# Graph attention over two layers: a chunk's exponentials added by DMA before one summing matmul, and a different pace for layer 1

## The chip, the cores and the metric

The kernel runs on one core of a Trainium2 chip. The metric is the device time of one launch in microseconds. The core has five engines with their own instruction queues, each worked off in order: TensorE (PE, with its weight loads shown as PEld), VectorE (DVE), ScalarE (ACT), GpSimd (POOL) and SyncE (SP), which here only issues DMAs. They meet through semaphores. TensorE writes into PSUM; all other data lies in SBUF, and DMAs move it between SBUF and the device's memory, or within SBUF.

## What is computed

The input is x (8 graphs of 2048 nodes with 256 features) and one adjacency matrix adj of 2048 x 2048. Layer 0 is masked multi-head attention with 4 heads of 64, in chunks of 256 keys, followed by two normalisations. Layer 1 is a graph attention layer with one head. Cut to what matters:

```python
# layer 0; scores in chunks of 256 keys, softmax over each chunk by itself
scores = einsum('bhnd,bhjcd->bhnjc', q, kc) / sqrt(64)
scores = where(mask == 0, -10.0, clip(scores, -10.0, 10.0))
attn = softmax(scores, axis=-1)            # over the 256 keys of one chunk
ctx = einsum('bhnjc,bhjcd->bhnd', attn, vc)  # added up over the chunks
out = layernorm(ctx @ Wo.T + bo + x) * gamma + beta
h = layernorm(x + out)
# layer 1
Wh = h @ W
e = leaky_relu((Wh @ a1)[:, :, None] + (Wh @ a2)[:, None, :], 0.2)
attention = softmax(where(adj > 0 or i == j, e, -inf), axis=-1)
result = layernorm(h + elu(attention @ Wh))
```

Since each chunk of layer 0 has a softmax of its own, each chunk needs the sum of its 256 exponentials for every query and head, the inverse of that sum, and a multiplication of its 64 values per head by that inverse before it is added to the context.

## The kernel before

Everything is in float32, and the instructions of all engines are written out by hand in the order in which they run. The order is built in *beats*. One beat is one tile of 128 keys of layer 0 against a block of 512 queries; two beats are a chunk (`J`, with `half` 0 and 1), 8 chunks a block of queries, 4 blocks a batch (graph), 8 batches: 256 chunks, 512 beats. After them the loop at line 986 adds beats in which layer 1 runs alone; there are 592 in all.

A beat of layer 0 has, in the program's order:

- `begin_beat` (line 816): for the steps of layer 1 in flight, the exponential of the weights on ACT (727) and their addition into `acc` on GpSimd (736); then new steps are taken from `layer1()` as the credit allows, each with an addition on ACT (714); then line 718 on VectorE.
- the scores of two pairs of heads, `sc`, on TensorE (899) into two PSUM tiles of [128, 2, 512]; the clip and mask on VectorE (909); the exponentials `e` on ACT (912) into SBUF tiles of a pool with 8 buffers, four for a chunk.
- `middle_of_beat`: the mask of layer 1's edges on VectorE (723).
- for the chunk before (`prev`): in half 0 the sums ("part 2", with a matrix of ones) and the first 32 values of every head, in half 1 the other 32 values (928). Each part takes 8 matmuls, for 4 heads and 2 key tiles. In the trace each matmul is two records, so a part has 16. The four heads use 32 columns of the array each. ACT copies each result to SBUF (936, 942).
- the sums' chain: `ds` on ACT (942), a DMA that rearranges it into `dc` (944), the reciprocal on VectorE (950), a DMA to device memory (952), a broadcast DMA back into `r` (956), and two beats after the sums the multiplication of the values on VectorE (963) and the addition into `ctxT` on GpSimd (964). `agenda` holds what is to run at the end of which beat. In the first batch the chain is given longer (`early`).
- `end_beat` (842): layer 1's products on TensorE (746, 761 in the last batch), then one step of each generator in `ahead` and `fins`: the preparation of layer 1 for the next batch (`prelude`, with the row maxima of line 438), the end of layer 0 for a block (`fin`), the end of layer 1 for a block (`fin1`), projections.

A step of layer 1 is one tile of 128 keys against 512 queries; 16 steps are a block, four blocks a batch. `begin_beat` adds 1.5 to the credit (1.3 in the last batch of layer 0, 1.0 after it), keeps at most 2, and takes a step for each whole credit. When the next block isn't ready, `layer1()` yields `None` and no step is taken in that beat. A block thus takes about 10.7 beats (12.3 in the last batch). Layer 1 of a batch runs beside layer 0 of the next batches, once layer 0 has finished all its blocks: it is at work in 45 beats of 64, from beat 89 on.

The tiles `w` of the steps have five buffers, and `hx`, `hr` and `ex` of `fin1` one each. `fin1` loads `hr` when the block ends, scales and exponentiates in the next beat, takes the minimum and maximum, and adds `hr` on GpSimd in the beat after (600 to 611).

Of the kernel before, what the change touches and what calls it, by code (L numbers as in the profile page):

```python
# [28 lines left out]
def tile_adj_attention__then__gat(  # L29
# [62 lines left out]
    eight = ctx.enter_context(tc.tile_pool(name="eight", bufs=8))  # L92
# [136 lines left out]
    for n in range(2):  # L229
        t = one.tile([P, F], F32, tag=("hx", "ex")[n], name=f"a_bc{n}")  # L230
        nc.sync.dma_start(out=t, in_=a[n * F : (n + 1) * F, :].rearrange("f o -> (f o)").partition_broadcast(P))
        a_bc.append(t)
# [284 lines left out]
    def last_prelude(b):  # L517
# [35 lines left out]
        while "hT" not in st:  # L553
# [4 lines left out]
            if beat >= 2 * total + 2 and held is None:  # L558
                held = []
                for n in range(HT):  # L560
                    fr = eight.tile([P, 2, HN], BF16, tag="e", name=f"far{b}_{n}")
# [26 lines left out]
    def fin1(b, ib, hx, acc):  # L588

        hr = one.tile([P, TPB, F], F32, tag="hr", name=f"hr{b}_{ib}")  # L590
        nc.sync.dma_start(out=hr, in_=h_d[b, ib])
# [10 lines left out]
        ex = one.tile([P, TPB, F], F32, tag="ex", name=f"ex{b}_{ib}")  # L602
        nc.scalar.activation(ex, hx, AF.Exp, bias=shifts[:, 1:2])
        yield
        nc.vector.scalar_tensor_tensor(hx, ex, 1.0, hx, ALU.min, ALU.max)
        nc.gpsimd.tensor_add(hx, hx, hr)
# [6 lines left out]
    def fin1_last(b, ib, hx):  # L613
# [4 lines left out]
        ex = one.tile([P, TPB, F], F32, tag="ex", name=f"ex{b}_{ib}")  # L618
# [181 lines left out]

    l1 = layer1()
# [5 lines left out]
    credit = 0.0  # L807
    RATE, LAST_RATE = 1.5, 1.3
# [7 lines left out]
    def begin_beat(rate):  # L816
# [5 lines left out]
        credit = min(credit + rate, 2.0)  # L822
        while l1_live and credit >= 1.0:
            s = next(l1, False)
            if s is False:
                l1_live = False
            elif s is None:
                break
            else:
                credit -= 1.0  # L830
                lows.append(s)
                s.low()
        for s in leaking:
# [36 lines left out]

    prev = None
    mk0 = {}
    for J in range(total + 1):
# [4 lines left out]
        cur = {"b": b, "ib": ib, "j": j, "es": [], "ctxT": ctxT, "v": vs[min(b, B - 1)], "name": f"{b}_{ib}_{j}"}  # L878
        for half in range(2):
# [13 lines left out]
            begin_beat(RATE if b < B - 1 else LAST_RATE)  # L893
            if live:
                scs = []
# [14 lines left out]
                for hp in range(NPAIR):  # L910
                    e = eight.tile([P, 2, IB], F32, tag="e", name=f"e{b}_{ib}_{c}_{hp}")
                    nc.scalar.activation(e, scs[hp], AF.Exp)  # L912
                    cur["es"].append(e)
            middle_of_beat()

            early = J < NIB * NCH
            if prev is not None:
                if half == 0:

                    pool, tag = (one, "hr") if early and J % 3 == 2 else (two, "un")  # L920
                    prev["un"] = pool.tile([P, 2, IB], F32, tag=tag, name=f"un{prev['name']}")
                for part in ((2, 0), (1,))[half]:
                    m = ps_m.tile([P, IB], F32, tag="m", name=f"u{prev['name']}_{part}")
                    for i in range(2):
                        pc = 2 * prev["j"] + i
                        for h in range(H):
                            f0 = h * D + part * DH
                            nc.tensor.matmul(  # L928
                                m[h * DH : (h + 1) * DH, :],
                                prev["v"][pc // TPB][:, pc % TPB, f0 : f0 + DH] if part < 2 else ones[:, 0:DH],  # L930
                                prev["es"][2 * i + h // 2][:, h % 2, :],
                                start=(i == 0),
                                stop=(i == 1),
                            )
                    if part < 2:
                        nc.scalar.copy(prev["un"][:, part, :], m)  # L936
                    else:

                        ds = two.tile([P, IB], F32, tag="ds", name=f"ds{prev['name']}")
                        nc.scalar.copy(ds, m)  # L942
# [92 lines left out]
```

## Time and profile before

| | |
|---|---|
| median of 3 runs | 4392.25 us (4391.52 to 4399.52) |
| the profiled execution | 4387.29 us, span 4385.5 us |
| granted TensorE clock, mean | 0.98 |
| DMA | 415.63 MB, mean 95 GB/s, hardware queue 30.5% of 16 engines |
| last exponential of layer 0 | about 4115 us |

Line numbers in a profile's rows are those of the kernel. In a row of instructions, "out<-in" names the tiles written and read, "xN" the number of records, then come the busy time and the mean of one in ns, and what the engine sat idle for before them. A row of the sums over windows has the window's bounds and length, then busy time and records of each engine, the granted clock, the DMA engines' busy share and GB/s. A busy TensorE is not TensorE at its peak, since the ends of its pipelined matmuls are modelled.

### The profile page before, as it was taken

The numbers are of one execution on the slowest core, as the hardware profiler recorded it, in microseconds if no ns is written. First come the engines' busy times: TensorE is split into PE (matmuls) and PEld (weight loads), VectorE is DVE, ScalarE is ACT, GpSimd is POOL, SyncE is SP. The second block draws the span as 40 slices with busy tenths as digits, with TensorE's granted clock in tenths as the row PEclk, the third lists the DMA queues.
The fourth block names the chain that finished last, engine by engine and source line by source line (L and its number), as shares of the span: only waits on it lengthen the run. The fifth ranks groups of instructions, "written<-read, shape, count | busy, mean of one in ns | idle before, by whom it ended". The sixth has DMA issues, their size and how long they took to land. (4 is left out here: it accounts for less than half of the span.)

```text
span 4385.5 us, 61171 instructions
## 1 busy us (share of the span) xinstructions
PE 4064.2 (93%) x23053; PEld 1907.6 (43%) x23053; DVE 3417.7 (78%) x4530; ACT 2564.4 (58%) x3842; POOL 1760.5 (40%) x901
## 2 busy tenths in 40 slices
PE   8889989999999999999899999999999999899767
PEld 3223334454344534454344543445434454344456
DVE  5876589965998669976699766996579965888777
ACT  5655556665566556666566665566556665555546
POOL 0222235543455334444245442554325542354420
PEclk9999999999999999999999999999999999999889
DMA  5554232222332233321333223232232222322321
GB/s 166 182 163 149 71 115 86 83 73 89 99 90 81 64 107 102 100 75 51 105 102 98 74 74 105 85 95 78 70 106 85 89 78 67 115 83 80 123 73 58
DMA packets 257641, 415.63 MB, mean 95 GB/s; under 512 B 85440, under 2 KB 120512, under 8 KB 256448
## 3 DMA queue, kind: packets, MB, share of 16 engines
q1 hardware_dynamic: 257344, 411.71, 30.5%
q8 instruction: 181, 2.97, 0.3%
q14 instruction: 116, 0.95, 0.1%
HBM read 340.66 MB, written 68.88 MB: 93 GB/s over the span
## 5 line engine op out<-in xcount | busy, mean ns | idle before, releaser
L912 ACT ACTIVATE e<-sc 128x1024 f32<-128x1024 f32 x1024 | 1034.2, 1020 | 1049.9 <-DVE sc L909 1006.7
L909 DVE SCALAR_TENSOR_TENSOR sc<-sc,mk 128x1024 f32<-128x1024 f32 x1024 | 1206.7, 1223 | 538.3 <-PE sc L899 352.6
L899 PE MATMUL sc<-qT,kT 64*128 64x512 f32 x4096 | 1060.4, 633 | 86.7 <-ACT e L912 86.2
L964 POOL TENSOR_TENSOR ctxT<-ctxT,un 128x1024 f32<-128x1024 f32 x224 | 568.5, 2538 | 1145.3 <-DVE un L963 1007.0
L928 PE MATMUL u<-e,v 128*32 128x512 f32 x8192 | 980.9, 597 | 0.0
L746 PE MATMUL us<-wh,w 128*128 128x256 f32 x3584 | 878.6, 395 | 81.9 <-ACT w L727 60.4
L746 PEld LDWEIGHTS us<-wh,w 128*128 128x128 f32 x3584 | 667.7, 193 | 422.2 <-ACT w L727 110.7
L736 POOL TENSOR_TENSOR acc<-acc,w 128x512 f32<-128x512 f32 x392 | 601.7, 1535 | 544.9 <-ACT w L727 534.4
L899 PEld LDWEIGHTS sc<-qT,kT 64*128 64x128 f32 x4096 | 347.2, 189 | 611.6 <-ACT e L912 281.8
L718 DVE SCALAR_TENSOR_TENSOR w<-ab,sj,w 128x512 f32<-128x512 f32 x512 | 571.5, 1137 | 4.6 <-ACT w L714 4.5
L928 PEld LDWEIGHTS u<-e,v 128*32 128x32 f32 x8192 | 240.6, 110 | 659.7 <-issue 543.9
L928 PE MATMUL u<-e,ones 128*32 128x512 f32 x4096 | 497.5, 604 | 0.0
L723 DVE TENSOR_TENSOR w<-w,mk 128x512 f32<-128x512 f32 x512 | 458.6, 917 | 37.1 <-DMA mk<-mask 34.6
L438 DVE CUSTOM_DVE_ANT_0 fb<-sj_row,fb 128x1024 bf16<-128x1024 f32 x240 | 387.8, 1626 | 2.3 <-DMA fb<-far 2.3
L714 ACT ACTIVATE w<-ab,sj 128x512 f32<-128x512 f32 x512 | 352.2, 714 | 8.7 <-POOL acc L734 5.4
L727 ACT ACTIVATE w<-w 128x512 f32<-128x512 f32 x512 | 308.8, 629 | 75.9 <-DVE w L723 75.3
L936 ACT COPY un<-u 128x512 f32<-128x512 f32 x512 | 300.5, 587 | 66.5 <-PE u L928 57.6
L963 DVE TENSOR_TENSOR un<-un,r 128x1024 f32<-128x1024 f32 x224 | 278.1, 1242 | 42.2 <-DMA r<-rd 36.7
L928 PEld LDWEIGHTS u<-e,ones 128*32 128x32 f32 x4096 | 107.8, 110 | 356.5 <-issue 305.4
L950 DVE RECIPROCAL dc<-dc 128x16 f32<-128x16 f32 x256 | 63.9, 249 | 149.8 <-DMA dc<-ds 134.0
L942 ACT COPY ds<-u 128x512 f32<-128x512 f32 x256 | 148.5, 580 | 3.0 <-PE u L928 2.5
L349 POOL TENSOR_TENSOR y<-x,bo_bc 128x1024 f32<-128x1024 f32 x32 | 77.6, 2426 | 163.6 <-DMA x<-in_x_dram 103.0
(112 smaller groups left out, 3114.7 us busy)
## 6 DMA issues: line engine op xcount, KB each, us to landing
r<-rd SPq DMA_DIRECT2D x256, 256.0 KB
mk<-mask SPq DMA_DIRECT2D x120, 512.0 KB
fb<-far SPq DMA_DIRECT2D x240, 256.0 KB
xT_k<-in_xT_dram SPq DMA_DIRECT2D x32, 512.0 KB
raw<-in_adjT_dram SPq DMA_DIRECT2D x32, 512.0 KB
rawf<-in_adj_dram SPq DMA_DIRECT2D x32, 512.0 KB
x<-in_x_dram SPq DMA_DIRECT2D x32, 512.0 KB
h_d<-y SPq DMA_DIRECT2D x32, 512.0 KB
```

Of the source, the lines that this page charges most:

```text
L438: nc.vector.tensor_tensor_reduce(out=fb, in0=row, in1=fb, scale=1.0, scalar=2 * FAR * 0.999, op0=ALU.add, op1=ALU.max, accum_out=dst,)
L714: nc.scalar.activation(self.w, k["ab"][:, 1, :], AF.Identity, bias=k["sj"][:, 1, c : c + 1])
L718: nc.vector.scalar_tensor_tensor(self.w, k["ab"][:, 0, :], k["sj"][:, 0, c : c + 1], self.w, ALU.add, ALU.max)
L723: nc.vector.tensor_tensor(self.w, self.w, self.k["mks"][self.c // HT][:, self.c % HT, :], ALU.min)
L727: nc.scalar.activation(self.w, self.w, AF.Exp)
L736: nc.gpsimd.tensor_add(k["acc"], k["acc"], self.w)
L746: nc.tensor.matmul(k["us"][:, t, :], self.w[:, ts(t, P)], k["wh"][c // TPB][:, c % TPB, 0:F], start=(first and t % 2 == 0), stop=last, ski ...
L899: nc.tensor.matmul(sc[:, h, :], kTs[b][c // TPB][h * D : (h + 1) * D, hp, ts(c % TPB, P)], qT[h * D : (h + 1) * D, hp, :], start=True, sto ...
L909: nc.vector.scalar_tensor_tensor(scs[hp], scs[hp], -CLIP, cap, ALU.max, ALU.min)
L912: nc.scalar.activation(e, scs[hp], AF.Exp)
L928: nc.tensor.matmul(m[h * DH : (h + 1) * DH, :], prev["v"][pc // TPB][:, pc % TPB, f0 : f0 + DH] if part < 2 else ones[:, 0:DH], prev["es"] ...
L964: nc.gpsimd.tensor_add(p["ctxT"], p["ctxT"], p["un"])
```

## The change

Where layer 1 has steps in flight at the start of the two beats in which a chunk's values are made (`beside`), the two key tiles of its exponentials are added by two DMAs, issued from GpSimd, one for each pair of heads: `es[0] += es[2]`, `es[1] += es[3]`. They are issued after the second half of the chunk's values. The sum over keys is then made from the two resulting tiles with 4 matmuls instead of 8, at the start of a half 1 beat, two beats after the DMAs and three after the beat in which the sums were made before. The reciprocal and its two DMAs come in the middle of the beat after that, and the scaling two beats after the sums; `last_scaled` keeps the scalings of successive chunks in successive beats. Where layer 1 isn't at work, the sums stay in half 0, now after the first values, with 8 matmuls.

The tiles of the exponentials have fixed places: `e{J % 2}_{(half + J // 2) % 2}_{hp}`, eight in all as before. A chunk's half 0 takes the places of the half 1 tiles of the chunk two before, that is of the sources of the additions.

The credit is counted in thirds: 4 a beat beside layer 0, 3 after it, at most 6, and it is cleared when a block has ended or isn't ready. A block takes 12 beats. In all there are 594 beats.

The room in SBUF is shared out anew: `ds` has one buffer instead of two, `un` three instead of two, and `ex` of `fin1` takes the tile of `hr`, so that `hr` is loaded after `ex` has been read, and added one beat later. In `fin1_last`, `ex` takes the tile `x`.

```diff
-    eight = ctx.enter_context(tc.tile_pool(name="eight", bufs=8))
...
-        hr = one.tile([P, TPB, F], F32, tag="hr", name=f"hr{b}_{ib}")
-        nc.sync.dma_start(out=hr, in_=h_d[b, ib])
         yield
...
-        ex = one.tile([P, TPB, F], F32, tag="ex", name=f"ex{b}_{ib}")
+        ex = one.tile([P, TPB, F], F32, tag="hr", name=f"ex{b}_{ib}")
         nc.scalar.activation(ex, hx, AF.Exp, bias=shifts[:, 1:2])
         yield
         nc.vector.scalar_tensor_tensor(hx, ex, 1.0, hx, ALU.min, ALU.max)
+        hr = one.tile([P, TPB, F], F32, tag="hr", name=f"hr{b}_{ib}")
+        nc.sync.dma_start(out=hr, in_=h_d[b, ib])
+        yield
         nc.gpsimd.tensor_add(hx, hx, hr)
...
-    RATE, LAST_RATE = 1.5, 1.3
...
-        credit = min(credit + rate, 2.0)
-        while l1_live and credit >= 1.0:
+        credit = min(credit + thirds, 6)
+        while l1_live and credit >= 3:
             s = next(l1, False)
             if s is False:
                 l1_live = False
             elif s is None:
+                credit = 0
                 break
             else:
-                credit -= 1.0
+                credit -= 3
                 lows.append(s)
                 s.low()
+                if s.c == NT - 1:
+                    credit = 0
...
+    def sums(p):
+        m = p["m"] = ps_m.tile([P, IB], F32, tag="m", name=f"s{p['name']}")
+        tiles = 1 if p["added"] else 2
+        for i in range(tiles):
+            for h in range(H):
+                nc.tensor.matmul(
+                    m[h * DH : (h + 1) * DH, :],
+                    ones[:, 0:DH],
+                    p["es"][2 * i + h // 2][:, h % 2, :],
+                    start=(i == 0),
+                    stop=(i == tiles - 1),
+                )
+    def inverses(p, early):
+        nonlocal last_scaled
+        ds = one.tile([P, IB], F32, tag="ds", name=f"ds{p['name']}")
+        nc.scalar.copy(ds, p.pop("m"))
...
+        lag = 1 if early else 0
+        if p["added"] and live:
+            at(-(beat + 1), inverse)
+        else:
+            at(beat + lag, inverse)
+        last_scaled = max(beat + 2 + 2 * lag, last_scaled + 1)
+        at(last_scaled, scaled)
...
-            begin_beat(RATE if b < B - 1 else LAST_RATE)
+            early = J < NIB * NCH
+            if half == 0:
+                beside = prev is not None and live and bool(lows or edged or weighted)
+            if half == 1:
+                for p in unsummed:
+                    sums(p)
+            begin_beat(4)
+            if half == 1:
+                for p in unsummed:
+                    inverses(p, False)
+                unsummed = []
...
-                    e = eight.tile([P, 2, IB], F32, tag="e", name=f"e{b}_{ib}_{c}_{hp}")
+                    e = one.tile(
+                        [P, 2, IB],
+                        F32,
+                        tag=f"e{J % 2}_{(half + J // 2) % 2}_{hp}",
+                        name=f"e{b}_{ib}_{c}_{hp}",
+                    )
                     nc.scalar.activation(e, scs[hp], AF.Exp)
                     cur["es"].append(e)
+            for fn in agenda.pop(-beat, []) if beat else []:
+                fn()
             middle_of_beat()
             if prev is not None:
                 if half == 0:
-                    pool, tag = (one, "hr") if early and J % 3 == 2 else (two, "un")
-                    prev["un"] = pool.tile([P, 2, IB], F32, tag=tag, name=f"un{prev['name']}")
-                for part in ((2, 0), (1,))[half]:
...
+                    prev["un"] = three.tile([P, 2, IB], F32, tag="un", name=f"un{prev['name']}")
+                values(prev, half)
+                if half == 0 and not beside:
+                    sums(prev)
+                    inverses(prev, early)
+                if half == 1 and beside:
+                    for hp in range(NPAIR):
+                        nc.gpsimd.dma_start(out=prev["es"][hp], in_=prev["es"][NPAIR + hp], accum_op=ALU.add)
+                    prev["added"] = True
+                    unsummed.append(prev)
...
-        begin_beat(1.0)
+        begin_beat(3)
```

`values(p, part)` holds the matmuls of one part of the values and their copy, and `inverse` and `scaled` the same operations as before; `spread`, the broadcast DMA, is now the end of `inverse`.

## The prediction

> **What bounds the kernel now.** The page gives shares of the whole span; the stages are told apart by the sums over windows. The exponentials of line 912 count the beats, two to a beat, so the window from 1145 to 1541 us, with 90 of them, is 45 beats beside layer 1, and the next 130 us are 19 beats without it. The pair repeats every 64 beats.
>
> ```profile
> PE 4064.2 (93%) x23053; PEld 1907.6 (43%) x23053; DVE 3417.7 (78%) x4530; ACT 2564.4 (58%) x3842; POOL 1760.5 (40%) x901
> ...
> 1145.00:1541.00 396.00, 383.36 (x2158) 191.37 (x2151) 328.47 (x413) 240.95 (x363) 191.47 (x102) 1.00 0.27 81
> 1541.00:1671.00 130.00, 118.75 (x734) 44.70 (x730) 87.25 (x131) 74.81 (x114) 42.10 (x19) 0.99 0.34 106
> ...
> 3791.00:4113.00 322.00, 300.33 (x1726) 141.41 (x1718) 266.93 (x350) 188.77 (x288) 145.45 (x75) 0.98 0.28 84
> 4113.00:4386.00 273.00, 190.85 (x773) 147.08 (x771) 220.71 (x375) 139.12 (x237) 60.87 (x34) 0.85 0.26 87
> ```
>
> The columns are length, then PE, PEld, DVE, ACT and POOL busy. Beside layer 1 TensorE is busy 383.4 of 396 us (97%), VectorE 83%. Without layer 1 it is 118.75 of 130, or 6.25 us of TensorE a beat and 4.6 of VectorE (87.25/19). TensorE sets the time until 4113 us; only the tail, where layer 1 runs alone, waits for others. Within the first window the groups by form say what TensorE does:
>
> ```profile
> L746 PE MATMUL us<-wh,w 128*128 128x256 f32 x512 | 122.7, 389 | 5.4 <-ACT hx L773 2.9 <-ACT w L727 2.5
> L909 DVE SCALAR_TENSOR_TENSOR sc<-sc,mk 128x1024 f32<-128x1024 f32 x90 | 106.1, 1223 | 42.1 <-ACT w L727 24.0 <-PE sc L899 18.1
> L899 PE MATMUL sc<-qT,kT 64*128 64x512 f32 x360 | 91.3, 625 | 1.4 <-ACT e L912 1.4
> L912 ACT ACTIVATE e<-sc 128x1024 f32<-128x1024 f32 x90 | 90.7, 1020 | 85.1 <-DVE sc L909 81.4
> L928 PE MATMUL u<-e,v 128*32 128x512 f32 x719 | 86.0, 595 | 0.0
> L928 PE MATMUL u<-e,ones 128*32 128x512 f32 x356 | 43.0, 599 | 0.0
> ```
>
> The last row is the target: no idle before it, so each microsecond of it is on the path. The last view is the timeline where the new wait will fall.
>
> ```profile
> 1713.26 1.92 PE L928 MATMUL u<-e,v 128*32 128x512 f32 x16
> ...
> 1715.12 3.72 PE L746 MATMUL us<-wh,w 128*128 128x256 f32 x16
> ...
> 1718.67 3.60 PE L256 MATMUL pq<-xT_q,WT_q 128*128 128x512 f32 x8
> ...
> 1722.20 1.99 PE L899 MATMUL sc<-qT,kT 64*128 64x512 f32 x8
> ...
> 1724.72 2.15 ACT L912 ACTIVATE e<-sc 128x1024 f32<-128x1024 f32 x2 [0.60 <-DVE sc L909]
> ...
> 1729.72 1.99 PE L899 MATMUL sc<-qT,kT 64*128 64x512 f32 x8
> ```
>
> A chunk's second half of values ends at 1715.2 us; the next beat's exponentials start 9.5 us later, and the scores that need their PSUM buffers 14.5 us later.
>
> [...] No GpSimd DMA is in this trace (the queue list has the hardware queue and instruction fetch only), [...] the two edges of line 723 at 1725.73 took 4.85 us beside GpSimd additions, against 0.68 us for one at 1717.50.
>
> **The change part by part.** *Removed.* Over the kernel the sums are 497.5 us for 4096 records, 16 a chunk: 1.94 us. An added chunk keeps 8, so it saves 0.97 us. In the changed program's order GpSimd has 322 new DMAs, two for each of 161 chunks: 24 in each of six full phases, 17 in the last. That is 161 x 0.97 = 156 us of TensorE, all in the 97% stage.
>
> *Moved: layer 1.* At 4/3 steps a beat with the credit cleared, a block takes 12 beats, where it took about 10.7. Following the loop, a phase has 50 beats instead of 45, and 14 are left without layer 1. TensorE per 64 beats was 383.4 + 118.75 = 502.1 us and becomes 502.1 - 23.3 = 478.8. Its idle time was 12.6 and 11.3. Without layer 1 it goes with the beats, 11.3 x 14/19 = 8.3. Beside layer 1 VectorE has 328.5 + 5 x 4.6 = 351 us in a phase of about 401, 87% where it was 83%; the steps per beat are more even. Idle there is between 12.6 (nothing changes) and 40 (VectorE sets every second beat); I take 22, since both engines then stand near full and wait for one another. A cycle is 478.8 + 8.3 + 22 = 509 against 526, 17 us less; six make -102. The last phase saves 17 x 0.97 = 16.5 and loses 3.5 in the same way: -13. The tail gets two beats more (594 in all against 592), at 273/80 = 3.4 us: +7.
>
> *Added: the wait.* The half-0 exponentials of a chunk overwrite the second tiles of the chunk two before, which are the sources of its additions. ACT therefore waits for both DMAs; behind it are the copies of the values and the weights of the next beat, and behind those TensorE. The DMA may start when the second values end. From there to the next scores that need the buffers, TensorE has products for two beats (3 steps in two pairs of three, 2 in the third, 1.96 us each), scores 2.07, values 1.92 and sums 0.97: 10.8 or 8.9 us, less 1.0 for an exponential. So the second addition may land some 9.8 us after the values (7.8 in every third chunk), more where projections stand between.
>
> Its landing is not in the trace. [...] The other transfers hold 27% of the DMA engines, [...] hidden in two chunks of three, 0.8 late in the third, which is 161/3 x 0.8 = 43 us at worst; projections cover about half of these, so +22.
>
> *GpSimd.* [...] Behind them wait the additions of context and of weights; it is busy 191 of 396 us beside layer 1, [...] If the cover went, the five buffers of w would make ACT wait.
>
> *At nothing.* The DMA chain of the inverse gets a beat more between copy and reciprocal, before the edges instead of after; VectorE's waits for it (134 us in total, off the TensorE path now) can only shrink. The inverse's two stores and loads keep their order in SP's queue, but stand ahead of the far load of that beat, which waits for VectorE anyway. One ds buffer: its copy-out is a chunk old. Three un buffers for two: the scaling comes up to three beats later. The shared tag of ex and hr moves a load behind an exponential and the normalisation a beat later; with 12 beats a block that is covered. The e tags are the same eight tiles.
>
> Sum against the profiled execution's 4387.3 us: -102 - 13 + 7 + 22 = -86, so 4301. The median of the runs shown is 5 us above that execution: 4306.
>
> **Rivals.** *All of it is kept*: no idle is added and the additions land in time. -156 - 6 x 3 (idle of the lost beats) + 7 = -167, a median of 4225 at best, 4250 with small losses. For it: the even steps and the inverse's longer lead. Against: VectorE at 87%.
>
> *Another wait takes it*: each phase gains the 23 us again as waits between VectorE and TensorE (idle 45 of 400), and the time stays at 4380 to 4400. For it: line 909 already waits 42 us in a phase. Against: [...] the stretching of lines 718 and 723 does not grow.
>
> *Slower: the additions land late.* Place: ACT's first exponential of each even beat. The gain without lateness is 108 us, so it is used up at 108/161 = 0.67 us per chunk beyond the slack, a landing at about 10.2 us. At 12 us a chunk loses 2.2 us, or 4.2 in every third, 2.1 on average if projections cover some: +338 - 108, or 4622. At 15 us it is over 5000. For it: the rate of an accumulating DMA is unknown, both DMAs share engines with broadcasts of 256 KB, [...] Against: where projections stand between, the slack is longer, 14.5 us to the scores in the timeline above.
>
> *That the change does not do what it says* is excluded by the order: 322 DMAs in, the halved sums out.
>
> **How the numbers follow.** Forecast (4265 to 4350): 0.46. All kept: 0.14. Another wait: 0.11, half of it within 0.2%. Late additions: 0.29. What a measurement of this kernel can tell from no change is about 0.2%, 9 us. So faster 0.65, same 0.06, slower 0.29. The range is 4235 to 4540: it leaves out some 0.17 of the late cases and 0.03 of the best; the forecast's own range is 4265 to 4350.
>
> **What would show it.** In the profile after: the sums' group with 8 records per added chunk; TensorE busy near 3908 us; L1 windows of about 400 us for 50 beats. If the additions are late, the exponentials' group shows idle time before it ended by a DMA on e, and TensorE is well under 97%. If VectorE takes it, the clip's row waits less and TensorE's score rows wait for e or VectorE. Wrong would be a time over 4400 with no DMA wait on the exponentials.

## The result, and the profile after

| | before | after |
|---|---|---|
| median | 4395.1 us (4391.5 to 4399.5) | 4521.2 us (4510.4 to 4530.1) |
| ratio to before, 95% interval | 1 | 1.0282 (1.0270 to 1.0295) |
| mean granted TensorE clock | 0.98 | 0.96 |
| TensorE busy | 4064.2 us | 4045.9 us |

The changed kernel is 2.8% slower; 4306 us were forecast. The forecast had 156 us of TensorE work go. TensorE's busy time fell by 18 us, and its idle time rose by some 150. First the page of the changed kernel: the engines' busy time, the queue of the new DMAs, and the last column of the new DMA's row, the median from issue to landing.

```profile
PE 4045.9 (89%) x21765; PEld 1872.5 (41%) x21765; DVE 3329.3 (74%) x4530; ACT 2567.0 (57%) x3842; POOL 1997.3 (44%) x1223
...
q0 software_dynamic: 46368, 168.84, 20.3%
...
e<-e POOLq DMA_DIRECT2D x322, 512.0 KB, 6.6
```

The 322 additions are there, and 6.6 us is no late landing by itself. The sums over windows put the time in its place. The windows are one cycle of 64 beats (50 beside layer 1, then 14 without it) and the tail.

```profile
1200.00:1631.00 431.00, 403.12 (x2151) 194.85 (x2147) 336.59 (x437) 259.90 (x391) 235.27 (x153) 0.98 0.58 140
1631.00:1742.00 111.00, 94.19 (x546) 34.88 (x541) 69.01 (x108) 56.25 (x86) 33.97 (x15) 0.94 0.34 99
...
4223.00:4522.00 299.00, 198.14 (x805) 150.65 (x797) 223.03 (x384) 141.27 (x241) 60.89 (x37) 0.84 0.27 84
```

The cycle takes 542 us where it took 526 and where 509 were forecast. TensorE is busy for 403.1 + 94.2 = 497.3 of them (502.1 before, 478.8 forecast) and idle for 44.7 (23.9 before, 30.3 forecast). So both terms of the forecast failed: 18.5 us of busy time that did not go, and 14.4 us more idle. The DMA engines beside layer 1 are busy for 0.58 of the time instead of 0.27, and the stretch without layer 1 runs at a clock of 0.94 instead of 0.99. The groups of the changed kernel say who waits for the additions:

```profile
L1001 ACT ACTIVATE e<-sc 128x1024 f32<-128x1024 f32 x1024 | 1041.0, 1022 | 1199.9 <-DVE sc L992 867.2 <-DMA e<-e 265.0 <-DVE w L723 18.4
...
L896 PE MATMUL s<-e,ones 128*32 128x512 f32 x2808 | 398.0, 615 | 45.7 <-DMA e<-e 27.2 <-ACT un L888 16.3 <-DVE r L596 2.2
...
L1019 POOL DMA_DIRECT2D e<-e x322 | 285.3, 1023 | 100.8 <-PE u L881 98.6 <-issue 2.1
...
L255 PE MATMUL pk<-xT_k,WT_k 128*128 128x512 f32 x256 | 133.3, 657 | 52.1 <-ACT un L888 46.5
```

ACT's exponentials wait for the additions for 265 us in all (22 us of delay were forecast, 43 at worst). This is idle time of ACT, not yet time of the kernel; behind the exponentials in ACT's queue stand the copies that free the PSUM. The last row shows where TensorE meets them: the projections of line 255 wait 46.5 us for the copies of values (1.7 us in the kernel before). The timeline shows one such case, where the second half of a projection waits for the copy of the values behind two blocked exponentials:

```profile
1388.26 1.99 PE L746 MATMUL us<-wh,w 128*128 128x256 f32 x8
...
1389.58 1.02 ACT L1001 ACTIVATE e<-sc 128x1024 f32<-128x1024 f32 x1 [4.51 <-DMA e<-e]
...
1390.09 1.88 PE L255 MATMUL pk<-xT_k,WT_k 128*128 128x512 f32 x4
...
1393.56 1.02 ACT L1001 ACTIVATE e<-sc 128x1024 f32<-128x1024 f32 x1 [2.96 <-DMA e<-e]
...
1394.70 0.58 ACT L888 COPY un<-u 128x512 f32<-128x512 f32 x1
...
1395.34 1.98 PE L255 MATMUL pk<-xT_k,WT_k 128*128 128x512 f32 x4 [3.38 <-ACT un L888]
...
1397.26 1.06 PE L896 MATMUL s<-e,ones 128*32 128x512 f32 x8
```

But there are long waits of TensorE with no addition in them. This is the timeline of the changed kernel in a stretch without layer 1. SPq rows are DMA issues.

```profile
1674.88 0.34 SPq L420 DMA_DIRECT2D sj_row<-sj_d  x1
...
1675.27 0.90 SPq L429 DMA_DIRECT2D fb<-far  x2
...
1676.98 0.51 SPq L345 DMA_DIRECT2D x<-in_x_dram  x1
...
1677.58 0.56 SPq L918 DMA_DIRECT2D rd<-dc  x1
...
1685.35 2.34 POOL L348 TENSOR_TENSOR y<-x,bo_bc 128x1024 f32<-128x1024 f32 x1 [10.00 <-DMA x<-in_x_dram]
1685.41 0.55 SPq L920 DMA_DIRECT2D r<-rd  x1
1687.72 1.29 DVE L363 TENSOR_TENSOR y<-po,y 128x512 f32<-128x512 f32 x2 [10.59 <-POOL y L348]
...
1688.47 1.94 PE L881 MATMUL u<-e,v 128*32 128x512 f32 x8 [5.84 <-DVE y L363]
```

Layer 1's preparation has asked for its broadcast row and its far tiles just ahead of the load of x and of the inverse. The load of x takes some 8 us, GpSimd and then VectorE wait 10 us each, and TensorE 5.84 us. The eight matmuls of the values then take 1.94 us, as long as sixteen usually do: the granted clock from 1688.4 to 1691.9 us is 0.50. In the whole kernel the values wait 30.5 us in this way, and not at all in the kernel before.

### The profile page after: what moved, and what is told of

Same layout as the page of the kernel before. It is cut to its first block, busy times and chain, and to the rows that moved or that the text cites. A ratio compares the mean times of both kernels' runs of the same rounds, so it can differ in the third digit from the quotient of the medians.

```text
span 4521.5 us, 59527 instructions
## 1 busy us (share of the span) xinstructions
PE 4045.9 (89%) x21765; PEld 1872.5 (41%) x21765; DVE 3329.3 (74%) x4530; ACT 2567.0 (57%) x3842; POOL 1997.3 (44%) x1223
## 3 DMA queue, kind: packets, MB, share of 16 engines
q0 software_dynamic: 46368, 168.84, 20.3%
## 5 line engine op out<-in xcount | busy, mean ns | idle before, releaser
L982 PE MATMUL sc<-qT,kT 64*128 64x512 f32 x4096 | 1083.3, 645 | 136.5 <-ACT e L1001 136.1
L881 PE MATMUL u<-e,v 128*32 128x512 f32 x8192 | 1005.0, 609 | 34.5 <-DVE y L363 30.5
L736 POOL TENSOR_TENSOR acc<-acc,w 128x512 f32<-128x512 f32 x392 | 563.4, 1437 | 551.9 <-ACT w L727 542.9
L718 DVE SCALAR_TENSOR_TENSOR w<-ab,sj,w 128x512 f32<-128x512 f32 x512 | 500.5, 994 | 6.1 <-ACT w L714 6.0
L723 DVE TENSOR_TENSOR w<-w,mk 128x512 f32<-128x512 f32 x512 | 487.6, 969 | 4.0 <-DMA mk<-mask 1.3
L896 PE MATMUL s<-e,ones 128*32 128x512 f32 x2808 | 398.0, 615 | 45.7 <-DMA e<-e 27.2
L437 DVE CUSTOM_DVE_ANT_0 fb<-sj_row,fb 128x1024 bf16<-128x1024 f32 x240 | 358.1, 1502 | 6.4 <-DMA fb<-far 6.4
L1019 POOL DMA_DIRECT2D e<-e x322 | 285.3, 1023 | 100.8 <-PE u L881 98.6
L911 ACT COPY ds<-s 128x512 f32<-128x512 f32 x256 | 148.4, 580 | 90.1 <-PE s L896 40.1
L896 PEld LDWEIGHTS s<-e,ones 128*32 128x32 f32 x2808 | 81.0, 111 | 253.8 <-issue 169.4
L255 PE MATMUL pk<-xT_k,WT_k 128*128 128x512 f32 x256 | 133.3, 657 | 52.1 <-ACT un L888 46.5
```

The lines of the kernel that those rows point to most:

```text
L437: nc.vector.tensor_tensor_reduce(out=fb, in0=row, in1=fb, scale=1.0, scalar=2 * FAR * 0.999, op0=ALU.add, op1=ALU.max, accum_out=dst,)
L718: nc.vector.scalar_tensor_tensor(self.w, k["ab"][:, 0, :], k["sj"][:, 0, c : c + 1], self.w, ALU.add, ALU.max)
L723: nc.vector.tensor_tensor(self.w, self.w, self.k["mks"][self.c // HT][:, self.c % HT, :], ALU.min)
L736: nc.gpsimd.tensor_add(k["acc"], k["acc"], self.w)
L881: nc.tensor.matmul(m[h * DH : (h + 1) * DH, :], p["v"][pc // TPB][:, pc % TPB, f0 : f0 + DH], p["es"][2 * i + h // 2][:, h % 2, :], start= ...
L896: nc.tensor.matmul(m[h * DH : (h + 1) * DH, :], ones[:, 0:DH], p["es"][2 * i + h // 2][:, h % 2, :], start=(i == 0), stop=(i == tiles - 1),)
```

## The experiments

**The parts of the addition.** Four runs keep the changed kernel's order and alter the additions, or the pace.

```diff
# e1: no chunk is added
-                beside = prev is not None and live and bool(lows or edged or weighted)
+                beside = False
# e2: credit 1.5 (1.3, 1.0) as in the kernel before
-            begin_beat(4)
+            begin_beat(RATE if b < B - 1 else LAST_RATE)
# e3: the two DMAs go, the halved sums stay
-                        nc.gpsimd.dma_start(out=prev["es"][hp], in_=prev["es"][NPAIR + hp], accum_op=ALU.add)
# e4: the two DMAs add 64 of the 1024 columns
+                        nc.gpsimd.dma_start(out=a[:, :, 0:32], in_=c2[:, :, 0:32], accum_op=ALU.add)
```

> The changed kernel with its new pace, its buffers and its moved loads, but no chunk is added by DMA: all sums in half 0 with 8 matmuls. Theory (the additions' landing holds up ACT, and TensorE's clock drops in the waits that follow): close to before, 4370 to 4420 us, clock about 0.98. Rival (the new pace and the moved steps are what costs): 4480 us or more, at most 40 us better than the changed kernel's 4521.

Measured: 4525.4 us, 1.0292 (1.0274 to 1.0310).

> The changed kernel with the old pace of layer 1 (1.5 and 1.3 steps a beat, credit kept at a block's end), additions by DMA as in the change. Theory (landing): still slower than before, 4450 to 4530 us, ACT waiting over 150 us for DMA on e. Rival (pace): 4300 to 4400 us, since the halved sums are kept and the new pace is gone.

Measured: 4534.5 us, 1.0317 (1.0297 to 1.0337).

> The changed kernel without the two DMAs of a chunk: the sums are made from the first key tile alone, so half of each sum's terms are left out; all else stands where the change puts it. Theory (landing): 4230 to 4320 us, that is the 156 us of TensorE less a few waits, with the clock back at 0.98 or over. Rival (pace and moved steps): the DMAs cost nothing, so 4480 us or more.

Measured: 4432.4 us, 1.0085 (1.0058 to 1.0113).

> The changed kernel with each addition cut to 64 of its 1024 columns, so most of the second key tile is left out of the sums; the number of DMAs, their issue on GpSimd and their waits stay. Theory (landing, set by bytes): landing 3 to 4.5 us instead of 6.6, 4240 to 4350 us. Rival A (the issue on GpSimd, about 1 us each, is what costs): within 50 us of 4521. Rival B (pace): 4480 us or more.

Measured: 4445.5 us, 1.0118 (1.0098 to 1.0137).

e3 takes out the two DMAs and leaves the rest of the order as it is. So the additions cost the changed kernel 89 us: 76 for the bytes of the whole ones, and 13 that small ones still cost (e4), less than e3's own runs lie apart (4422.8 to 4448.9). But without the DMAs, and with the halved sums, the kernel is still 37 us slower than before, where the forecast was 108 us faster without lateness.

e1 has neither DMAs nor halved sums and is as slow as the changed kernel: 130 us over the kernel before. From e1 to e3 the halved sums, which also come later, give 93 us, not 156. On this path the additions take back what the shorter sums give, and no more. But e1 is not just the changed kernel without its additions: its inverses come earlier, and its layer 1 starts at beats 154, 218, 282 where the changed kernel has 156, 220, 284. The waits of TensorE differ with that. For the context at the output projection it waits 51.6 us in e1, and 20.8 in the changed kernel; at the values for line 363 it waits not at all in e1, 30.5 us in the changed kernel and 28.6 in e3. So the 130 us show what the order and the buffers can cost without an addition; they are not a part of the changed kernel's own loss that could be read off. In e2 the old pace makes the kernel 13 us slower still, so the new pace is not the cause in these surroundings. The groups of e3:

```profile
L1001 ACT ACTIVATE e<-sc 128x1024 f32<-128x1024 f32 x1024 | 1039.0, 1022 | 1023.5 <-DVE sc L992 975.8
...
L896 PE MATMUL s<-e,ones 128*32 128x512 f32 x2808 | 359.7, 610 | 11.2 <-ACT un L888 9.0
```

The wait on the additions is gone from ACT's row and from the sums' row, and the sums themselves are busy 359.7 us instead of 398.0.

**The surroundings, one by one in the kernel before.**

```diff
# e5: the new pace, with its cleared credit
-            begin_beat(RATE if b < B - 1 else LAST_RATE)
+            begin_beat(4)
# e6: values before sums
-                for part in ((2, 0), (1,))[half]:
+                for part in ((0, 2), (1,))[half]:
# e7: ex and hr share a tile, hr is loaded later and added a beat later
-        ex = one.tile([P, TPB, F], F32, tag="ex", name=f"ex{b}_{ib}")
+        ex = one.tile([P, TPB, F], F32, tag="hr", name=f"ex{b}_{ib}")
# e12: e5 and e7 together
```

> The kernel before with the new pace alone (thirds, credit cleared). After the first four runs the additions cannot be the main cause, since the change without them takes 4525 us. Theory A (the new pace costs): 4460 us or more. Theory B (the order of values and sums, or the shared tile of ex and hr, costs): 4370 to 4410 us.

Measured: 4406.9 us, 1.0017 (1.0007 to 1.0027).

> The kernel before with the sums after the first half of the values instead of ahead of them. Theory B1 (the sums' chain starts 1.9 us later, and VectorE waits for dc in line): VectorE's wait for dc<-ds rises from 134 to over 200 us and the time to 4430 us or more. If this order is harmless: 4385 to 4405 us.

Measured: 4442.8 us, 1.0108 (1.0091 to 1.0124).

> The kernel before with ex and hr of the end of layer 1 in one tile, so that hr is loaded later and added a beat later. Theory B2 (GpSimd waits in line for hr's load, and the context's addition behind it holds up the projection of the output): 4420 us or more, with GpSimd waiting over 20 us for hr<-h_d. If it is harmless: 4385 to 4405 us.

Measured: 4399.2 us, 1.0004 (0.9995 to 1.0013).

> The kernel before with the new pace and with ex and hr in one tile, nothing else (un and ds keep their buffers). The pace alone took 4407 us, the shared tile alone 4399, and the change without additions and with the sums first 4502. Theory (with blocks of 12 beats the end of layer 1 falls a beat later into the loads of the next preparation, so that the store of the output, the broadcast of the key row and the inverse's DMAs stand in one queue): 4470 us or more. Rival (the buffers of un and ds, and the tiles of the exponentials, make the 95 us): 4395 to 4425 us.

Measured: 4435.1 us, 1.0098 (1.0081 to 1.0114).

e6: the sums' chain begins a set of values later, and its copy comes to VectorE later. The group of the reciprocals in e6 has idle time ended by that DMA of 237.0 us, 134.0 before:

```profile
L950 DVE RECIPROCAL dc<-dc 128x16 f32<-128x16 f32 x256 | 63.8, 249 | 259.7 <-DMA dc<-ds 237.0 <-issue 22.7
```

Behind the reciprocal in VectorE's queue stand the clips of the next beat. e7 and e12 are a warning: the shared tile costs nothing alone and 0.8% beside the new pace. Why they add up so is open.

**Sums first, in the changed kernel.** e9 and e10 put the sums of chunks that are not added ahead of their values, as in the kernel before; e9 adds none. e8 and e11 make both parts of an added chunk's values in half 0, so that the additions may start a beat earlier.

```diff
# e10; e9 has beside = False as well
-                values(prev, half)
                 if half == 0 and not beside:
                     sums(prev)
                     inverses(prev, early)
+                values(prev, half)
# e8; e11 on top of e10, with the sums kept three beats after the DMAs
-                values(prev, half)
+                if half == 0 or not beside:
+                    values(prev, half)
+                if half == 0 and beside:
+                    values(prev, 1)
```

> The changed kernel with both halves of an added chunk's values in half 0, so that the two additions start a beat earlier and have about 8 us more to land. Theory (the additions' landing is a cost of about 60 us beside the other cause): ACT's wait for e<-e nearly gone (265 us in the change), 4440 to 4480 us. Rival (the other transfers and the issue on GpSimd cost, not the landing): within 25 us of 4521.

Measured: 5820.8 us, 1.3241. In this kernel the sums follow one beat after the DMAs instead of two. TensorE waited 928 us for the additions at its sums. It shows what an early sum costs and nothing else.

> The first experiment's kernel (the change without additions) with the sums ahead of the first half of the values again. Theory (the order of sums and values is what cost, by the later inverse): what is left is the new pace, so 4395 to 4425 us, VectorE's wait for dc<-ds below 150 us. Rival (the new buffers and tiles cost as well): 4440 us or more.

Measured: 4501.8 us, 1.0243 (1.0228 to 1.0258). That is in the rival's range: of e1's 130 us the order of sums and values makes 24, and 107 are left.

> The change with its additions, and the sums ahead of the values wherever a chunk is not added. Theory: the chunks beside layer 1 are not touched by this, and 95 of 256 get their old chain back: 4440 to 4490 us. Rival (the chunks not added do not matter beside the additions' waits): within 15 us of 4521.

Measured: 4513.4 us, 1.0267 (1.0244 to 1.0291). That is 8 us below the changed kernel, within the spread of both. In the changed kernel this order costs nothing that can be told.

> As the run before, and both halves of an added chunk's values in half 0, so that the additions are issued a beat earlier; the sums stay where the change has them, now three beats after the additions. (The earlier run with the values together had let the sums come one beat after the additions, which it should not have.) Theory (the landing costs some 60 to 90 us by ACT's waits): 30 to 80 us below the run before, ACT's wait for e<-e under 60 us. Rival (the cost beside layer 1 is the added traffic and the issue on GpSimd, not the landing): within 20 us of the run before.

Measured: 4653.3 us, 1.0586. ACT no longer waits for the additions, and the kernel is 140 us slower than e10. The longest wait of TensorE in e11:

```profile
PE sc L982 <- ACT e L1001: 196.9, 90, 6.3
```

TensorE waits for the exponentials at the scores, 90 times and 196.9 us in all (136.1 in the changed kernel). Two parts of values in one half and none in the other make beats of unequal length, which fits the first, but no run shows it by itself. Both expectations were wrong: removing the wait in this way cost more than the wait.

**The beat at which layer 1 starts.** From e12 (4435) to e9 (4502) there remained three un buffers, one ds, the fixed places of e, and one thing that only the order of the program shows: `last_scaled + 1` scales the last chunk of the first batch a beat later. Layer 1 then starts at beat 90 instead of 89, and since each batch's layer 1 has to end before the preparation of the next can take its tile `wh`, at 154 and 218 instead of 153 and 217. (In the changed kernel, where the last chunk is an added one, at 156 and 220.)

```diff
# e13: e9 with the beat given back
-        last_scaled = max(beat + 2 + 2 * lag, last_scaled + 1)
+        last_scaled = max(beat + 2 + 2 * lag, last_scaled + (0 if beat == 2 * NIB * NCH else 1))
# e14: the kernel before, last chunk of a batch scaled a beat later
-                        at(beat + 2 + 2 * lag, scaled)
+                        late = 1 if beat and beat % (2 * NIB * NCH) == 0 else 0
+                        at(beat + 2 + 2 * lag + late, scaled)
# e15: the changed kernel, the same
+        late = 1 if p["added"] and p["ib"] == NIB - 1 and p["j"] == NCH - 1 else 0
+        last_scaled = max(beat + 2 + 2 * lag + late, last_scaled + 1)
# e16: e10 with e13's edit, and
+                if prev is not None and prev["ib"] == NIB - 1 and prev["j"] >= NCH - 3:
+                    beside = False
# e17: the kernel before, layer 1 of a batch held back by two beats
-                while ib not in st["ab"] or beat < st["ab"][ib][0]:
+                while ib not in st["ab"] or beat < st["ab"][ib][0] + (2 if ib == 0 else 0):
# e18: e16 without the two DMAs of an added chunk
```

> No additions, sums ahead of the values as in e9, but the first batch's last chunk is scaled in the same beat as in the kernel before, so that layer 1 starts at beats 89, 153, 217 and so on instead of 90, 154, 218. Its instructions then stand in the order of e12's on every engine and only buffers differ (three un, one ds, fixed tiles for e). Theory, the 67 us from e12 to e9 are the beat at which layer 1 starts: about 4435 us (4425 to 4450). Rival, they are the buffers: about 4500 us (4490 to 4510). In between: both.

Measured: 4438.3 us, 1.0099 (1.0082 to 1.0116). Without additions it is the beat: 63 us. The buffers cost nothing that can be told.

> The kernel before with one edit: the last chunk of each batch is scaled one beat later, so that layer 1 starts at beats 90, 154, 218 instead of 89, 153, 217; 594 beats. Theory, starting on a beat that is a first half costs time by itself: 4430 us or more. Rival, only together with the new pace or the shared tile does it cost: 4392 to 4410 us (two beats more of the tail are 7 us).

Measured: 4579.9 us, 1.0417 (1.0401 to 1.0433).

> The kernel before with one edit: layer 1 of each batch is held back by two beats and starts at beats 91, 155, 219; 594 beats. Its beats with two steps are second halves of a chunk, as in the kernel before; in e14 they were first halves. Theory, it is the half that costs in e14: 4395 to 4420 us. Rival, it is the lateness, or the place of layer 1 against the blocks of layer 0: 4500 us or more.

Measured: 4386.9 us, 0.9981 (0.9974 to 0.9988).

e14, with layer 1 one beat later, is 184 us slower than the kernel before; e17, with layer 1 two beats later, is the only version a little faster. The two also differ in how: e14 moves the scaling of a batch's last chunk, e17 holds layer 1 back and leaves the scaling alone. TensorE's waits at the scores, first in the kernel before, then in e14 and e17, follow the half and not the lateness:

```profile
L899 PE MATMUL sc<-qT,kT 64*128 64x512 f32 x4096 | 1060.4, 633 | 86.7 <-ACT e L912 86.2
```

```profile
L899 PE MATMUL sc<-qT,kT 64*128 64x512 f32 x4096 | 1083.7, 643 | 172.7 <-ACT e L912 171.8
```

```profile
L899 PE MATMUL sc<-qT,kT 64*128 64x512 f32 x4096 | 1060.7, 632 | 87.9 <-ACT e L912 87.6
```

These 86 us are the largest part of the 120 us by which e14's idle time grows. At the output projection the wait for the context grows by 25 us more, which may come from the later scaling itself; holding layer 1 back by one beat with the scaling left alone was not run. Half-clock periods grow from 180 to 325 us. The timeline of TensorE in the kernel before shows why the half counts. Sixteen records of line 746 are two steps of layer 1, eight are one; a row of `u<-e,ones` marks the half with the sums.

```profile
1203.82 1.99 PE L899 MATMUL sc<-qT,kT 64*128 64x512 f32 x8
1205.74 1.92 PE L928 MATMUL u<-e,v 128*32 128x512 f32 x16
1207.59 3.72 PE L746 MATMUL us<-wh,w 128*128 128x256 f32 x16
1211.24 1.99 PE L899 MATMUL sc<-qT,kT 64*128 64x512 f32 x8
1213.16 1.93 PE L928 MATMUL u<-e,ones 128*32 128x512 f32 x16
1214.90 1.90 PE L928 MATMUL u<-e,v 128*32 128x512 f32 x16
1216.73 1.99 PE L746 MATMUL us<-wh,w 128*128 128x256 f32 x8
```

The beat without the sums has two steps, the beat with the sums one: 7.4 us of TensorE in each, 1203.82 to 1211.24 and on to 1218.66. A rate of 1.5 with a start on an odd beat locks the two together; in the program's order all 136 beats with two products beside layer 0 are second halves. The same view of e14, where they are first halves:

```profile
1317.27 1.99 PE L899 MATMUL sc<-qT,kT 64*128 64x512 f32 x8
1319.19 1.92 PE L928 MATMUL u<-e,v 128*32 128x512 f32 x16
1321.04 1.99 PE L746 MATMUL us<-wh,w 128*128 128x256 f32 x8
1324.45 2.26 PE L899 MATMUL sc<-qT,kT 64*128 64x512 f32 x8 [1.42 <-ACT e L912]
1326.64 1.92 PE L928 MATMUL u<-e,ones 128*32 128x512 f32 x16
1328.38 1.90 PE L928 MATMUL u<-e,v 128*32 128x512 f32 x16
1330.21 3.72 PE L746 MATMUL us<-wh,w 128*128 128x256 f32 x16
```

Now TensorE has 5.8 us in one beat and 9.4 in the other. In the short one it is done before ACT's exponentials have freed the scores, and waits 1.42 us. The windows of e14's cycle:

```profile
1188.00:1603.00 415.00, 388.42 (x2175) 192.27 (x2171) 332.76 (x416) 240.87 (x364) 190.37 (x102) 0.99 0.25 77
1603.00:1741.00 138.00, 120.71 (x718) 46.22 (x714) 84.56 (x129) 74.19 (x113) 40.48 (x19) 0.94 0.33 101
```

The 45 beats beside layer 1 take 415 us instead of 396, the 19 without it 138 instead of 130. At 4/3 steps a beat there is no such lock: a pattern of 1, 1, 2 against chunks of two beats, with two steps in 54 first and 54 second halves. The beat at which layer 1 starts costs there too (63 us from e13 to e9), for a reason that the timeline of e9 shows in part:

```profile
1659.49 0.33 SPq L420 DMA_DIRECT2D sj_row<-sj_d  x1
...
1661.46 0.48 SPq L918 DMA_DIRECT2D rd<-dc  x1
...
1668.27 0.55 SPq L920 DMA_DIRECT2D r<-rd  x1
...
1674.81 1.23 DVE L927 TENSOR_TENSOR un<-un,r 128x1024 f32<-128x1024 f32 x1 [6.25 <-DMA r<-rd]
...
1676.18 2.34 POOL L928 TENSOR_TENSOR ctxT<-ctxT,un 128x1024 f32<-128x1024 f32 x1 [18.02 <-DVE un L927]
...
1678.57 1.65 PE L356 MATMUL po<-WT_o,ctxT 128*128 128x256 f32 x3 [9.54 <-POOL ctxT L928]
```

The broadcast row of layer 1's preparation is issued 2 us before the inverse of the chunk that ends a block. The load follows its store by 6.8 us, where 1.5 is the median of the kernel; the two take 13 us together, and the output projection, which needs that chunk, waits 9.54 us. TensorE has seven such waits over 1.7 us ahead of the output projection in e9, 54.8 us in all, against 16.4 us in e13: 38 of the 63 us. That the large load delays the small ones is read from their order; no run shows it by itself. The rest is spread over other waits.

> The changed kernel with one edit: an added last chunk of a batch is scaled one beat later still, so that from the second batch on layer 1 starts at beats 157, 221, 285 (odd, as in the kernel before) instead of 156, 220, 284; 595 beats. Theory, it is the half of the chunk in which layer 1 starts: 4450 to 4480 us although everything is later by a beat. Rival, it is only how late it starts: 4521 us and up to 10 more.

Measured: 4639.3 us, 1.0551 (1.0535 to 1.0567). In this kernel, by the program's order, the last chunk of a batch is scaled after its un buffer has been taken by the chunk three later, so the scaling works on a tile that no longer holds its values alone. The theory fell: layer 1 on odd beats is 118 us slower than the changed kernel, not faster. So it is not the half alone; the place of layer 1's blocks against those of layer 0, or the shared buffer, counts. Holding layer 1 back by one beat in the changed kernel with the scaling left alone was not tried, so this stays open.

> The changed kernel with the sums ahead of the values in chunks that are not added (as e10), the last three chunks of each batch not added (284 DMAs instead of 322), and the beat given back as in e13, so that layer 1 starts at 89, 153, 217 and so on; 590 beats. Theory: the additions give nothing net, so about e13's time, 4420 to 4450 us. Rival, the start doesn't matter: about e10's 4513 us less some us for the fewer additions, 4495 to 4515. In neither case faster than the kernel before.

Measured: 4507.3 us, 1.0254 (1.0239 to 1.0270). The profile has 298 DMAs, so 149 chunks are added; the 284 expected were a miscount. The rival held: with additions the earlier start (and 12 added chunks fewer) gives back 6 us of e10's 4513, within its spread, where it gave 63 without them.

> e16 without its two DMAs a chunk; the halved sums stay and read the two tiles that are not added to, so half of the terms of these sums is left out. Theory, the additions take what they took in the changed kernel (89 us, from e3): 4410 to 4430 us, so that even free additions are no gain over the kernel before in these surroundings. Rival, the shorter sums give their 93 us from e13's time too: 4340 to 4360 us, and the additions take 150 us or more.

Measured: 4449.3 us, 1.0127 (1.0108 to 1.0147). From e13 to e18 the shorter and later sums of 149 chunks, without any DMA, cost 11 us instead of giving something; the additions cost 58 more. Neither expectation had that. And e18, which starts layer 1 at 153 like e13, is 17 us slower than e3, which starts it at 156: beside halved sums the earlier start is no gain (the two differ in 12 chunks and in the order of the sums not halved as well). The windows of e13 and then of e18 in the same cycle:

```profile
1150.00:1586.00 436.00, 418.44 (x2347) 201.99 (x2343) 348.70 (x441) 261.08 (x393) 200.54 (x106) 0.98 0.28 82
1586.00:1689.00 103.00, 92.34 (x542) 35.43 (x538) 69.90 (x105) 55.48 (x85) 32.66 (x14) 0.95 0.32 98
```

```profile
1156.00:1587.00 431.00, 405.55 (x2163) 196.92 (x2159) 333.53 (x436) 260.62 (x391) 191.70 (x104) 0.97 0.27 81
1587.00:1693.00 106.00, 92.47 (x558) 35.09 (x554) 74.05 (x110) 56.47 (x87) 37.31 (x16) 0.97 0.36 105
```

TensorE's busy time falls by 12.8 us a cycle (510.8 to 498.0), where the sums that go (22 chunks by 0.97) are worth 21; its idle time rises by 10.8 (28.2 to 39.0). What was freed became waiting; by which wait is open.

**The sum of the steps.** Put in a row, the runs lead from the kernel before to the changed one:

| kernel | ratio to before | what the step adds |
|---|---|---|
| e5: the new pace | 1.0017 | +0.17% |
| e12: ex and hr in one tile | 1.0098 | +0.81% |
| e13: buffers of un, ds and e | 1.0099 | +0.01% |
| e9: layer 1 a beat later | 1.0243 | +1.44% |
| e1: values before sums | 1.0292 | +0.49% |
| e3: halved sums, later in the order, and later starts | 1.0085 | -2.07% |
| the changed kernel: the two DMAs | 1.0282 | +1.97% |

The order of the steps matters (e6 cost 1.08% by itself, e7 nothing; the start cost 1.44% without additions and nothing that can be told with them, e10 and e16), so this is one path, not a price list.

## Why the prediction was wrong

Three terms of the sum were off, all the same way, 212 us together. Along the path kernel before, e1, e3, changed kernel: layer 1's new pace with its idle time, the tail and all that was put at nothing came to +48 us in the forecast and +130 in e1; the sums removed were -156 and gave -93; the wait for the additions was +22 and took 89.

*At nothing.* This is the step that failed most, by 82 us. It costed the moved inverse chain, the scaling "up to three beats later", the shared tile and the buffers at zero. The buffers are free (e13). Without additions the rest was not: the shared tile took 0.8% beside the new pace, values before sums 0.5% to 1.1% (e1, e6), and the later scaling 1.4% (e9 against e13), because it is also what releases the next layer 1. How the loss is shared out in the changed kernel itself stays open: there neither the order (e10) nor the start (e16) gives much back. The step said that VectorE's waits for the inverse's DMA, "off the TensorE path", "can only shrink"; in the chunks that are not added the copy comes later, and in e6 they grew from 134 to 237 us and the kernel by 1.1%. And it found the order in SP's queue kept, but did not ask what else is on the DMA engines at that beat.

*Removed.* The instructions went as counted. But 0.97 us a chunk was the price of sums in an unbroken stream. Alone, between other shapes, the eight records take 1.06 us (timeline of the changed kernel), and the gain without DMAs was 93 us from e1 to e3 and none from e13 to e18, not 156. The prediction took each microsecond of the sums to be on the path; in e18 most of what was freed turned into waiting.

*Moved: layer 1.* The 50 and 14 beats came as followed from the loop. The idle time beside layer 1 was 27.9 us where 22 was taken, inside the bounds of 12.6 and 40. Without layer 1 it was 16.8 where 8.3 was taken, since no wait was expected there. "The steps per beat are more even" was wrong: evenness that counts is TensorE's time per beat, and the old pace had it with the sums included (e14). What the new pace lost alone was small (e5).

*Added: the wait.* That ACT waits, and TensorE behind its copies, was right. The lateness behind the price, 0.8 us in every third chunk, was an assumption of the author's: no trace had shown how long an adding DMA takes. Here it landed 6.6 us from its issue, with 4.5 and 11.7 as ends. The price was too small: 89 us (e3 against the changed kernel), not 22. The slack was counted up to the scores that need the buffers, but TensorE stops earlier, at a projection whose PSUM tile waits for a copy behind the exponential (46.5 us, against 26.2 in e3). And the sums were not counted at all: they stand idle 27.2 us for the additions, and are busy 38 us longer than in e3. The rival of late additions named ACT's exponentials as the place, but from a landing of over 10 us; the median stayed below.

*GpSimd.* Right: its busy time beside layer 1 rose from 191 us to 235, the issues take 0.92 us at the median, the stretching of lines 718 and 723 did not grow (988.1 us busy together, 1030.1 before), and ACT's waits for GpSimd at w (5.6 us in the kernel before) are gone rather than grown. The reading that an edge of line 723 takes 0.68 us without GpSimd's additions beside it was not clean: at 1717.49 us, as that edge began, GpSimd began two additions as well.

*Tail.* The two beats were worth +7 us. The window of the last stretch is 26 us longer than before: layer 1 of the last batch but one starts three beats later and has three beats fewer beside layer 0, so more of it is left for the tail.

*The clock.* No step had it. The trace's clock records have 34 periods at half clock, 180 us, in the kernel before and 64, 362 us, after. At a clock of 0.50 eight records of the values took 1.94 us (1688.47 us in the changed kernel), at a clock of 1.00 sixteen took 1.92 us (1205.74 us in the kernel before). So the 181 us more are, as an estimate, up to 90 us of TensorE time. In the cycle shown they can account for most of the 18.5 us that did not go: 27.3 us at half clock after, 6.8 before, which is up to 10 us; and sums that take 31.3 us beside layer 1 where 0.97 for each eight of their 200 records would be 24.2, another 7. The two overlap, since some of the longer sums are at half clock. The sign in "wrong would be a time over 4400 with no DMA wait on the exponentials" was not met: the time was over 4400, but the wait was there, and the additions were a part of the loss and not the whole.

## What to carry to other kernels

Before a step is costed at nothing because it has slack, find what it releases: here the last scaling of a batch releases layer 1, and one beat of delay in the first batch moved every later one. Where two periodic schedules run side by side, count the bound engine's time in each beat with both of them in it: their phase can be worth more (184 us between the kernel before and e14) than the work that a change removes. And to decide between a cost in the new operation and a cost in what was moved for it, run the new order without the new operation first, and look whether the rest of the schedule then stays in place: in e3 it did, in e1 layer 1 moved by two beats.

## What the runs showed of the hardware

TensorE's clock fell after short waits. In the clock records of the traces before and after, the periods at half clock are 3.41 us or multiples of it, but for one at each kernel's end, and within a trace they all begin on one grid of 3.413 us. In the kernel before, a single wait of 1.8 us, ended at 1649.4 us, was followed by such a period from 1650.5 us on. Busy time and clock of the 3.40 us ahead of it and of the next 3.40 us:

```profile
1647.10:1650.50 3.40, 1.58 (x12) 0.30 (x4) 3.37 (x5) 2.93 (x5) 2.42 (x2) 0.99 0.49 133
1650.50:1653.90 3.40, 3.40 (x13) 0.90 (x16) 3.33 (x5) 0.42 (x1) 2.27 (x1) 0.50 0.18 65
```

The stretches of that grid can be counted. In the two traces each of the 98 periods began at the end of a stretch in which TensorE's records leave about 1.7 us idle or more; and of 109 stretches with 2.0 us idle or more, up to the start of the last period of each trace, 108 were followed by half clock. So such a wait was paid twice here: at a clock of 0.50 a period of 3.41 us does, as an estimate, 1.7 us less work. (The ends of matmuls are modelled, so the border between 1.7 and 2.0 us is not sharp.)

An adding DMA of 512 KB took GpSimd 0.92 us at the median to issue. Cut to 64 of 1024 columns, its issue rose to 1.43 us on average from 1.02, while the landing fell from 6.6 to 3.1 us. So this smaller adding DMA was dearer for GpSimd and cheaper for those who wait. It takes two separate pieces of each partition, and the packets of its queue rose from 46368 to 87584, which may be why the issue is longer; no run separates the pieces from the size.
